# Half of a product behind the next pair's first, transposes one product earlier, an average one step later, seven more tiles of x stored

## The chip, the cores and the metric

The kernel runs on one core of a Trainium2 chip. The metric is the device time of one launch in microseconds (us): the median of several runs. A profiled execution of the same program gives the trace. The core has five engines that run side by side and wait for each other by semaphores: TensorE (PE, matmuls; PEld are its weight loads), VectorE (DVE), ScalarE (ACT), GpSimd (POOL, which here issues the indirect DMAs) and SyncE (SP, which here issues plain DMAs). Each engine takes its instructions in the order in which the program lists them.

## The reference

Sixteen graphs of 1024 nodes with 512 features; one adjacency matrix for all. Attention with 8 heads of 64 over the neighbours of each node, an output projection, a residual sum and a normalisation of each row:

```
q = (x @ Wq + bq).reshape(b, n, H, HD)
k = (x @ Wk + bk).reshape(b, n, H, HD)
v = (x @ Wv + bv).reshape(b, n, H, HD)
scores = jnp.einsum('bqhd,bkhd->bhqk', q, k) / jnp.sqrt(jnp.float32(HD))
scores = scores + (1.0 - adj)[None, None, :, :] * -1000000000.0
attn = jax.nn.softmax(scores, axis=-1)
out = jnp.einsum('bhqk,bkhd->bqhd', attn, v).reshape(b, n, d)
y = out @ Wo + bo
...
x = _layernorm(x + y, axis=-1)
```

x is (16, 1024, 512) and adj is (1024, 1024), zeros and ones, all float32. Most nodes have only a few neighbours; a node with none gets the mean of all v rows of its graph, since its scores are all equally masked.

## The kernel before

**Rows in order of their number of neighbours.** At its start the kernel sorts the 1024 nodes by number of neighbours, and from then on works on x in that order: eight tiles of 128 rows for each graph (a "batch" b), tile t of batch b being number 8b + t. Rows of x come by an indirect DMA on POOL (`gather_x`, L1009).

**Two streams of work.** The first, the *fronts*, is dense and bound to TensorE: it turns x into q, k and v and writes them to DRAM. The second is sparse. For every tile of queries it goes through *blocks*: for each block POOL gathers 128 rows of k and v, one for each query (L1292), VectorE multiplies q with k and sums by head (L1313, L1317), ScalarE takes the exponentials (L1328), ScalarE or VectorE weighs v (L1341, L1345), and the result is added up (L1357, or on TensorE L1366, L1367). There are 530 blocks in all. When a tile is closed, VectorE divides (L1387), TensorE transposes the result o (`turn`, L1401), ScalarE copies it out (L1405), TensorE multiplies it with Wo (`finish`, product po, L799), and then come the residual and the normalisation (`complete`, L1097).

**Steps.** The program is written out by a planner in plain Python, the loop from L1538. One turn of it is a *step*, n, and belongs to one block. `later(k, fn)` puts a piece of work k steps on, and within a step work is written out in a fixed order: exponentials, products, gathers, sums, then what was planned for that step (`plan`), then the *units* of TensorE. Units are taken from the list `finishing` (products po) if there is one, else from `fronts`, while a credit lasts that each step tops up (L1592 to L1618). A unit has a cost, a function, and a condition on which it may be written out; if it isn't ready, the step ends. The list `urgent` holds small TensorE work that goes out in each step after its first unit, as long as there are fronts: the turns of o, and `mean_pe`.

**A pair of tiles.** `pair(b, j)` (L816) makes the front units of tiles 2j and 2j + 1. q is a plain product of four matmuls for each tile (`q0`, `q1`); tile 1 has no q except in the first batch, and tile 0's is made once for two batches. k and v of the two tiles come from a scheme with seven products of half the size in place of eight, on sums and differences of the weights (T1 to T4, made once) and of x (s1 to s4, four VectorE sums L783 to L786 for each pair, `combine`; s1, s2, s3 have one buffer each). The products share three kinds of PSUM banks: x and z have one bank each, p4, p6 and p7 take from a ring of four banks that q, po, the turns and the transposes of x use too. A half of a product is two matmuls, and each float32 matmul shows as two instructions in the trace: a half is "x4". In the order of L994 to L1005:

- x, first half; ScalarE copies it out as e (L969)
- p6; VectorE makes w = p6 + e (L972)
- q of the even tile
- x, second half, on top of the first; ScalarE copies it out as k of the even tile (L835)
- p7; VectorE makes g = p7 + w (L975)
- xt: the transposes of x for the next pair (L757); ScalarE copies them out in the next step (L761), and a step later come the four sums
- z, first half (below: z1); VectorE makes v of the odd tile, v1 = z + g (L984)
- q of the odd tile
- p4; VectorE makes k of the odd tile (L979), and its k and v go to DRAM
- z, second half (below: z2), on top of z1; it may be written out once v1 has been; VectorE makes v of the even tile, v0 = z + w (L988), and its k and v go to DRAM

When both tiles have been sent, VectorE adds their v to a sum (`add_v`, L863). After the last pair of a batch `mean_pe` (L867) averages the sum with one matmul, ScalarE copies the row, SP stores it (L873), and the batch is marked as set up; only then are its blocks gathered.

**Rows stored twice.** The residual of a tile is x itself, in sorted order. For tiles whose numbers are in `STORED`, the x that was loaded for the fronts is written to DRAM (L773, on SP) and loaded from there as the residual (L1035, SP); then the load of x three tiles on, which takes the same buffer, is planned two steps later (L774). For the others the residual is gathered again by POOL (L1038), and the load of x three tiles on follows at once. `SPILL` names tiles whose turned o is put to DRAM and multiplied with Wo at the end.

Of the kernel before, what the change touches and what calls it, by code (L numbers as in the profile page):

```python
# [42 lines left out]
LAZY = 2  # L43

SPILL = (*(8 * b + t for b in range(4, 12) for t in (3, 6)), 45, 69, 93, 102, 103, 106, 107)
STORED = {*SPILL, *(i for i in range(10, 102) if i % 8 in (2, 4, 5, 7)), *(i for i in range(102, 128) if i % 8 > 1)}
LATE = 12

AHEAD_LAST = 11
# [129 lines left out]
def kernel(  # L179
# [75 lines left out]
    with ExitStack() as main:  # L255
# [190 lines left out]
        now, plan, rest, urgent, known, waiting, combined = [0], {}, {}, [], [], [], []  # L446

        def later(k, fn):
            plan.setdefault(now[0] + k, []).append(fn)
# [366 lines left out]
        def pair(b, j):  # L816
# [16 lines left out]
            def out_k(i, p):  # L833
                kv = new_kv(i)
                nc.scalar.copy(kv[:, 0:D], p)  # L835
                later_last(1, lambda: norm(b, tt[i], kv[:, 0:D]))
# [5 lines left out]
            def send(i):  # L842
                assert b < PAIRED_FROM or gathered[0] >= start[max(0, b // 2 * 2 - 2)]
                kv = KV[b, tt[i]]
                rows, base = kv_of(b)
                for lo, hi in ((0, LONE), (LONE + P, 2 * P)) if b and tt[i] == 0 else ((tt[i] * P - (LONE if b and tt[i] == 1 else 0), None),):
                    hi = lo + P if hi is None else hi
                    part = slice(0 if lo % P == 0 or hi - lo == P else LONE, P if hi - lo == P or lo else LONE)
                    later(1, lambda lo=lo, hi=hi, part=part: nc.sync.dma_start(rows[base + lo:base + hi, :], kv[part, :]))
                R["sent"] = R.get("sent", 0) + 1  # L850
                if R["sent"] == 2:
                    later(1, add_v)
                    if j == NT // 2 - 1:
                        later(2 if b else 3, lambda: urgent.append(mean_pe))

            def add_v():
                kv = [KV.pop((b, t))[:, D:] for t in tt]
# [64 lines left out]
            if (b, j) == (0, 0):  # L922
# [12 lines left out]
                units = q0 + q1 + xt  # L935
# [9 lines left out]
            def a(i, h):  # L945
                return XT[b, tt[i]][:, ts(h, HD2)]
# [44 lines left out]
            def s(i):  # L991
                return lambda: SX[b, j][i - 1]
# [3 lines left out]
            units += unit("p6", s(2), T2, True, out_w, None)  # L996
            units += q0
            units += unit("x", lambda: a(0, 1), B21, False, lambda: out_k(0, R["x"]), "e")
            units += unit("p7", s(3), T3, True, out_g, None)
            units += xt  # L1000
            units += unit("z", s(1), T1, True, out_v1, None)
            units += q1
            units += unit("p4", lambda: a(1, 1), T4, True, out_k1, None)
# [512 lines left out]
        with tc.manual_schedule():  # L1516

            fronts += transpose_x(0, 0) + transpose_x(0, 1)
            fronts_by = []
            for b in range(B):  # L1520
                for j in range(NT // 2):
                    fronts += pair(b, j)
                fronts_by.append(sum(u[0] for u in fronts))
            fronts_time = fronts_by[-1]

            def needed(b, part):
                b += int(part)
                if b >= B:
                    return fronts_time
                return fronts_by[b - 1] + (part - int(part)) * (fronts_by[b] - fronts_by[b - 1])  # L1530

            finishing, last_finish, reloads, last_reload = [], -LEAD_IN, 0, 0
            fronts_end = start[B - 1] - 12
            credit = 0.0
            for t in range(3):
                load_x(0, t)
            n = -LEAD_IN
            while n < total or plan or rest or urgent or done or finishing or spilled or lone_tiles or not guarded:  # L1538
                now[0] = n
                if n < 0:  # L1540
                    share = START_SHARE if n > FRONT_BY else LEAD_SHARE if n > -LEAD_IN else TRANSPOSE * 1.5
                elif n >= start[LATE + 1]:

                    share = sum(u[0] for u in fronts) / max(fronts_end - n, 1) + NS * SUM / NBT if fronts else LAST_SHARE
                elif n in start:

                    b = start.index(n)
                    left = sum(u[0] for u in fronts)
                    ahead = EARLY + FIRST * (1 - max(0, b - 1) / LATE)
                    goal = fronts_time - needed(b + 2, ahead / NBT)  # L1550
                    kept = sum(number(b, t) not in SPILL for t in tiles_of(b))
                    share = (max(0.0, left - goal) + kept * NPAIR * PRODUCT + NS * SUM) / (start[b + 1] - start[b])
                if 0 <= n + 3 < total:
                    exponentials(n + 3)
                if 0 <= n + 4 < total:
                    products(n + 4)
                while gathered[0] < min(n + (AHEAD if fronts else AHEAD_LAST) + 1, total) and blocks[gathered[0]][0] in set_up:
                    gather(gathered[0])
                    gathered[0] += 1
                if 0 <= n + 1 < total and not by_act(n + 1):  # L1560
                    weigh(n + 1)
                if 0 <= n < total and blocks[n][2] < OWN[blocks[n][1]]:
                    add_own(n)
                if 0 <= n + 4 < total:
                    scores(n + 4)
                if n - 1 in closes:
                    normalise(*closes[n - 1])
                if 0 <= n < total and blocks[n][1:] == one_key_at(blocks[n][0]):
                    turn(blocks[n][0], ONE_KEY, V1.pop(blocks[n][0]))
                if 0 <= n < total and blocks[n] == (B - 1, *MORE_AT):  # L1570
                    turn(B - 1, MORE_TILE, V1.pop("more"))
                for fn in plan.pop(n, ()):
                    fn()
                if 0 <= n + 2 < total and by_act(n + 2):
                    weigh(n + 2)
                for fn in rest.pop(n, ()):
                    fn()
                credit += paced(share, n) if n >= 0 else share
                if 0 <= n < total and blocks[n][2] >= OWN[blocks[n][1]]:
                    add_up(n)  # L1580
                    credit -= SUM
                for tile_done in done[:0 if fronts and len(done) < LAZY else 1 if fronts else 2] + coming:
                    if tile_done not in loaded and kept_y() < 5:
                        load_y(*tile_done)
                if lone_tiles and kept_y() < 4:
                    load_lone(lone_tiles.pop(0))
                coming[:] = [t for t in coming if t not in loaded]
                if spilled and not fronts and n > last_reload + 1 and len(Y) - kept_y() < 7:
                    reload(*spilled.pop(0), reloads)
                    reloads, last_reload = reloads + 1, n  # L1590
                first_unit = True
                while credit > 0 or urgent:  # L1592
                    if urgent and not (first_unit and fronts):
                        urgent.pop(0)()
                        continue
                    if (
                        not finishing and len(done) > (LAZY if fronts else 0) and n > loaded.get(done[0], n) + 1
                        and n > last_finish + bool(fronts) and not total - 2 <= n < total
                    ):
                        finishing = finish(*done.pop(0))  # L1600
                        last_finish = n
                    units = finishing or fronts
                    if not units:
                        if urgent:
                            urgent.pop(0)()
                            continue
                        break
                    cost, fn, ready = units[0]
                    if ready and not ready():
                        if urgent:  # L1610
                            urgent.pop(0)()
                            continue
                        break
                    del units[0]
                    fn()
                    credit -= cost
                    first_unit = False
                credit = min(credit, 2 * share)  # L1618
                while known and waiting:
                    load_x(*waiting.pop(0))  # L1620
                preps += prep.pop(n, [])
                preps = [g for g in preps if next(g, True) is None]
                n += 1
# [34 lines left out]
```

## Time and profile before

| what | value |
|---|---|
| runs | 1843.5, 1845.46 and 1851.71 us; median 1845.46 |
| profiled execution, its own time | 1842.18 us |
| its span in the trace | 1840.4 us, 25352 instructions |
| granted TensorE clock, mean | 0.996 |
| DMA | 558.54 MB, mean 303 GB/s |

How to read it: the span runs from the first to the last instruction of the trace; the time of the launch lies a little above it. "Busy" is the time in which an engine had an instruction under way. Matmuls overlap in the pipeline, so one shows as 0.59 us while the next starts 0.43 us after it. The slices of the page show TensorE at nine tenths or more from the second slice to the last but one:

```profile
PE   7999999999999999999999999999999999999997
...
DVE  6889889999989999999999999999999999997986
ACT  3637869989889898999889988989799999987886
POOL 1367766766565776767757666677666767665786
```

Each digit is a fortieth of the span, 46 us, in tenths. The costliest groups of TensorE in the page, with count, busy time, mean ns and idle time before them:

```profile
L799 PE MATMUL pq<-wq,xT 128*128 128x512 f32 x792 | 367.8, 596 | 0.0
L799 PE MATMUL po<-wo,oT 128*128 128x512 f32 x792 | 359.3, 594 | 0.7 <-ACT oT L1405 0.7
L956 PE MATMUL x<-b,xT 128*128 128x512 f32 x504 | 237.3, 593 | 0.5 <-ACT e L969 0.4
L956 PE MATMUL pp<-t,s 128*128 128x512 f32 x504 | 237.0, 593 | 0.0
L956 PE MATMUL z<-b,s 128*128 128x512 f32 x252 | 119.2, 596 | 7.0 <-DVE kv L984 7.0
L956 PE MATMUL z<-t,s 128*128 128x512 f32 x252 | 118.6, 593 | 0.0
```

In these names pq and po are the products of q and of the output, pp are p4, p6 and p7, z<-t,s is z1 and z<-b,s is z2, pxT are the transposes of x, poT the turns of o, pm the averages.

### The profile page before, as it was taken

To read this page: it belongs to the slowest core of one execution; us is meant where nothing else is said; L and a number is where in the kernel's file an instruction comes from. 1 tells how busy PE (TensorE), PEld (TensorE's weight loads), DVE (VectorE), ACT (ScalarE), POOL (GpSimd) and SP (SyncE) were. 2 spreads that over 40 slices of the span, in tenths; PEclk is the share of its full clock that TensorE was granted. 3 is DMA by queue.
4 is the path that set the end of the run, shared out by engine and by line. 5 is a ranking of instruction groups with operands and counts; after the bars stand their busy time and mean duration, and the time that the engine had idled before them with its cause. 6 is when DMAs were issued, how large, how long until landed. Compare 5 with 4: busy or idle time off the path is not lost.

```text
span 1840.4 us, 25352 instructions
## 1 busy us (share of the span) xinstructions
PE 1798.2 (98%) x5140; PEld 876.2 (48%) x5140; DVE 1693.7 (92%) x3473; ACT 1563.2 (85%) x6183; POOL 1215.3 (66%) x1142
## 2 busy tenths in 40 slices
PE   7999999999999999999999999999999999999997
PEld 3444454554444454444444445444544444444443
DVE  6889889999989999999999999999999999997986
ACT  3637869989889898999889988989799999987886
POOL 1367766766565776767757666677666767665786
PEclk9999999999999999999999999999999999999998
DMA  7358787989889899999988998999989999889995
GB/s 287 106 190 253 256 325 237 346 301 327 308 280 314 295 336 319 344 316 308 347 316 310 346 335 276 343 321 322 339 315 325 314 355 326 306 324 325 338 319 191
DMA packets 198791, 558.54 MB, mean 303 GB/s; under 512 B 33450, under 2 KB 33470, under 8 KB 198626
## 3 DMA queue, kind: packets, MB, share of 16 engines
q0 software_dynamic: 112640, 370.50, 59.3%
q1 hardware_dynamic: 82910, 180.52, 26.2%
q10 hardware_dynamic: 3076, 5.82, 0.9%
q14 instruction: 122, 1.00, 0.2%
q8 instruction: 43, 0.70, 0.2%
HBM read 420.30 MB, written 157.45 MB: 314 GB/s over the span
## 4 chain that ended last, share of the span: by engine, by line
PE 69%; DVE 10%; ACT 9%; DMA 4%; issue 3%; POOL 1%; SPq 0%; POOLq 0%; DVEq 0%; ACTq 0%
PE po L799 17%; PE pq L799 15%; PE pp L956 12%; PE z L956 9%; PE x L956 9%; ACT pv L1341 5%; DVE qk L1313 2%; PE poT L1401 2%; PE pxT L757 2%; PE sum L1367 2%; DVE s L1317 2%; PE sum L1366 2%; DVE pv L1357 1%; ACT sq_k L809 1%; DMA kvg<-kv_pair,place_row 1%
## 5 line engine op out<-in xcount | busy, mean ns | idle before, releaser
L1341 ACT ACTIVATE pv<-kvg,pv 128x64 f32<-128x64 f32 x3600 | 907.5, 341 | 0.0
L1292 POOL DMA_INDIRECT kvg<-kv_pair,place_row x462 | 526.7, 1140 | 307.4 <-ACT pv L1341 99.6
L799 PE MATMUL pq<-wq,xT 128*128 128x512 f32 x792 | 367.8, 596 | 0.0
L1317 DVE TENSOR_REDUCE s<-qk 128x8 f32<-128x512 f32 x530 | 360.7, 681 | 6.8
L799 PE MATMUL po<-wo,oT 128*128 128x512 f32 x792 | 359.3, 594 | 0.7 <-ACT oT L1405 0.7
L1313 DVE TENSOR_TENSOR qk<-qt,kvg 128x512 f32<-128x512 f32 x434 | 297.2, 685 | 1.1 <-DMA kvg<-kv_rows,key_row 0.6
L956 PE MATMUL x<-b,xT 128*128 128x512 f32 x504 | 237.3, 593 | 0.5 <-ACT e L969 0.4
L956 PE MATMUL pp<-t,s 128*128 128x512 f32 x504 | 237.0, 593 | 0.0
L1357 DVE TENSOR_TENSOR pv<-pv,pv 128x520 f32<-128x520 f32 x329 | 228.3, 694 | 4.3 <-ACT pv L1341 4.2
L799 PEld LDWEIGHTS po<-wo,oT 128*128 128x128 f32 x792 | 149.1, 191 | 170.0 <-issue 160.2
L799 PEld LDWEIGHTS pq<-wq,xT 128*128 128x128 f32 x792 | 148.4, 192 | 161.9 <-issue 149.9
L1010 POOL DMA_INDIRECT x<-in_x_dram,asked_row x120 | 133.0, 1108 | 77.8 <-issue 21.3
L1148 POOL DMA_INDIRECT out_dram<-y,asked_row x129 | 146.9, 1139 | 39.1 <-issue 21.2
L1328 ACT ACTIVATE pv<-s,absent 128x8 f32<-128x8 f32 x434 | 127.0, 294 | 44.0 <-DVE s L1317 40.8
L809 ACT ACTIVATE sq_k<-kv 128x128 bf16<-128x128 f32 x512 | 150.8, 301 | 6.4 <-DVE kv L979 3.4
L956 PEld LDWEIGHTS pp<-t,s 128*128 128x128 f32 x504 | 94.7, 191 | 108.1 <-issue 99.4
L956 PEld LDWEIGHTS x<-b,xT 128*128 128x128 f32 x504 | 94.2, 191 | 107.4 <-issue 99.0
L956 PE MATMUL z<-b,s 128*128 128x512 f32 x252 | 119.2, 596 | 7.0 <-DVE kv L984 7.0
L1246 POOL DMA_INDIRECT qg<-q_rows,query_row x96 | 104.4, 1088 | 28.4 <-issue 26.9
L956 PE MATMUL z<-t,s 128*128 128x512 f32 x252 | 118.6, 593 | 0.0
L956 PE MATMUL pp<-t,xT 128*128 128x512 f32 x252 | 118.5, 593 | 0.0
L1134 ACT ACTIVATE y<-y,stats 128x512 f32<-128x512 f32 (+1 forms) x128 | 102.7, 806 | 17.0 <-DVE stats L1129 17.0
(279 smaller groups left out, 2713.0 us busy)
## 6 DMA issues: line engine op xcount, KB each, us to landing
kv_pair<-kv SPq DMA_DIRECT2D x98, 512.0 KB
q_rows<-q SPq DMA_DIRECT2D x106, 256.0 KB
qt<-q_rows SPq DMA_DIRECT2D x98, 256.0 KB
residual<-x SPq DMA_DIRECT2D x83, 256.0 KB
y<-residual SPq DMA_DIRECT2D x83, 256.0 KB
kv_rows<-kv SPq DMA_DIRECT2D x15, 512.0 KB
kvg<-kv_pair,place_row POOLq DMA_INDIRECT x462, 6.9
kv_pair<-kv SPq DMA_DIRECT2D x28, 256.0 KB
```

The source lines that it names most:

```text
L799: nc.tensor.matmul(p, lhs(c), w[:, c, :], start=(c == 0), stop=(c == NPAIR - 1))
L809: nc.scalar.activation(sq, s[:, ts(h, P)], AF.Square, scale=scale, accum_out=sums[:, h:h + 1])
L956: nc.tensor.matmul(R[bank], l[:, ts(c, P)], right[:, c, :], start=(first and c == 0), stop=(c == 1), skip_group_check=True,)
L1010: nc.gpsimd.indirect_dma_start(out=y, out_offset=None, in_=x_rows, in_offset=bass.IndirectOffsetOnAxis(ap=asked_row[:, t:t + 1], axis=0), ...
L1148: nc.gpsimd.indirect_dma_start(out=out_rows[b, t], out_offset=bass.IndirectOffsetOnAxis(ap=rows, axis=0), in_=y, in_offset=None, element_o ...
L1246: nc.gpsimd.indirect_dma_start(out=q, out_offset=None, in_=q_rows[b % ROWS], in_offset=bass.IndirectOffsetOnAxis(ap=rows, axis=0))
L1292: nc.gpsimd.indirect_dma_start(out=KG[n], out_offset=None, in_=rows, in_offset=bass.IndirectOffsetOnAxis(ap=(place_row if b else key_row)[ ...
L1313: nc.vector.tensor_tensor(QK[n], q, KG[n][:, 0:D], op=OP.mult)
L1317: nc.vector.tensor_reduce(S[n], QK.pop(n).rearrange("p (h d) -> p h d", d=HD), axis=AX.X, op=OP.add)
L1328: nc.scalar.activation(PV[n][:, D:], S.pop(n), AF.Exp, bias=bias)
L1341: nc.scalar.activation(pv[:, ts(h, HD)], v[:, ds(D + h * HD, HD)], AF.Copy, scale=pv[:, D + h:D + h + 1])
L1357: nc.vector.tensor_tensor(PV[b, t], PV[b, t], pv, op=OP.add)
```

## The change

Five edits, all in the planner. The number of matmuls is the same.

1. z2 of a pair is kept back (`held`) and put behind the first unit (the first half of x) of the next pair. The very first pair, which has other units, is put in whole; the last pair's z2 comes at the end.
2. xt stands ahead of p7 rather than behind it.
3. `mean_pe` goes to the urgent list three steps after the last pair's tiles have been sent, in every batch; before, it was two steps in all but the first.
4. With fronts left, urgent work goes out after two units of a step rather than after one.
5. `STORED` has all tiles from 10 on except tiles 0 and 1 of each batch. Numbers 11, 14, 19, 22, 27, 30 and 99 are new; there are 90 in place of 83.

```
-STORED = {*SPILL, *(i for i in range(10, 102) if i % 8 in (2, 4, 5, 7)), *(i for i in range(102, 128) if i % 8 > 1)}
+STORED = {*SPILL, *(i for i in range(10, 128) if i % 8 > 1)}
...
                     if j == NT // 2 - 1:
-                        later(2 if b else 3, lambda: urgent.append(mean_pe))
+                        later(3, lambda: urgent.append(mean_pe))
...
             units += unit("x", lambda: a(0, 1), B21, False, lambda: out_k(0, R["x"]), "e")
+            units += xt
             units += unit("p7", s(3), T3, True, out_g, None)
-            units += xt
             units += unit("z", s(1), T1, True, out_v1, None)
...
-            fronts_by = []
+            fronts_by, held = [], []
             for b in range(B):
                 for j in range(NT // 2):
-                    fronts += pair(b, j)
+                    head, *tail = pair(b, j)
+                    fronts += [head] + held + (tail if (b, j) == (0, 0) else tail[:-1])
+                    held = [] if (b, j) == (0, 0) else tail[-1:]
                 fronts_by.append(sum(u[0] for u in fronts))
-            fronts_time = fronts_by[-1]
+            fronts += held
+            fronts_time = sum(u[0] for u in fronts)
+            fronts_by[-1] = fronts_time
...
-                first_unit = True
+                ahead = 2 if fronts else 0
                 while credit > 0 or urgent:
-                    if urgent and not (first_unit and fronts):
+                    if urgent and ahead <= 0:
                         urgent.pop(0)()
                         continue
...
-                    first_unit = False
+                    ahead -= 1
```

## The prediction

> **What bounds the kernel now.** I read the page's first part, then TensorE's list of waits, then the timelines around the longest of them.
>
> ```profile
> PE 1798.2 (98%) x5140; PEld 876.2 (48%) x5140; DVE 1693.7 (92%) x3473; ACT 1563.2 (85%) x6183; POOL 1215.3 (66%) x1142
> ```
>
> TensorE stands still for 1840.4 - 1798.2 = 42.2 us in all. The change moves TensorE's instructions and drops none, so what it can gain is inside these 42.2 us. Its waits:
>
> ```profile
> PE pxT L757 <- DMA x<-in_x_dram: 7.1, 2, 4.2
> PE z L956 <- DVE kv L984: 7.0, 5, 3.0
> PE pm L867 <- DVE vsum L863: 3.1, 3, 1.9
> PE poT L1401 <- DVE stats L1123: 3.1, 1, 3.1
> PE poT L1401 <- DVE o L1387: 2.6, 1, 2.6
> ...
> PE x L956 <- ACT e L969: 0.4, 1, 0.4
> PE pxT L757 <- DMA x<-in_x_dram,asked_row: 0.4, 1, 0.4
> ```
>
> Columns: total, times, longest. The first is the very beginning of the run and the fourth its very end (1808 us); the change touches neither. Lines two, three and five are what it can reach: 7.0 + 3.1 + 2.6 = 12.7 us, 0.7% of the time.
>
> The five waits of z are the second half of product z (z2), which needs VectorE's v1 (L984) to have emptied the one z bank. Pair by pair in the timeline, four of the five are the first pair of a batch, where the odd tile has no q product, so only p4 (1.72 us) stands between z1 and z2. One of them on TensorE, then on VectorE:
>
> ```profile
> 542.96 1.88 PE L956 MATMUL z<-t,s 128*128 128x512 f32 x4
> 544.68 1.88 PE L956 MATMUL pp<-t,xT 128*128 128x512 f32 x4
> 546.39 0.59 PE L1366 MATMUL sum<-pv,sums 128*128 128x256 f32 x2
> 546.83 0.61 PE L1367 MATMUL sum<-pv,sums 128*128 128x264 f32 x2
> 549.82 1.55 PE L956 MATMUL z<-b,s 128*128 128x512 f32 x3 [2.38 <-DVE kv L984]
> ```
>
> ```profile
> 544.95 0.43 DVE L783 TENSOR_TENSOR s<-xT 128x256 f32<-128x256 f32 x1 [2.96 <-PE z L956]
> ...
> 546.08 0.42 DVE L786 TENSOR_TENSOR s<-xT,s 128x256 f32<-128x256 f32 x1
> 546.42 0.69 DVE L1112 TENSOR_TENSOR y<-po,y 128x512 f32<-128x512 f32 x1
> ...
> 549.08 0.68 DVE L984 TENSOR_TENSOR kv<-z,g 128x512 f32<-128x512 f32 x1
> ```
>
> The four sums of x for the next pair (L783 to L786) overwrite s1, which z1 still reads (one buffer), so VectorE waited 2.96 us for z1, and v1, queued behind them, came late for z2.
>
> **The change part by part.** A product of four matmuls takes 1.72 us from its start to the next one's (542.96 to 544.68). A step is one gathered block: 434 + 96 = 530 of them (L1313) from 120.8 to 1808.3 us, 3.2 us each.
>
> Half of z behind the next pair's x: z2 gets 1.72 us more cover in every pair but the first and the last. Two waits are longer: 3.01 us (at 1065.88) leaves 1.29, 2.38 leaves 0.66; the other three vanish. Saved 7.0 - 1.95 = **5.05**. Ends: 0 (VectorE is later by as much) and 7.0. The price is that v0 (L988), the even tile's store and the sum of v come 1.72 us later.
>
> Average of v at three steps in place of two: the matmul that averages comes 3.2 us later, and its longest wait was 1.9, so **3.1** is saved. Ends 0 and 3.1. Late next is the store of the mean row, and the gathers of that batch, which are released by it. They run many steps ahead except in the last batch:
>
> ```profile
> 1680.77 0.24 SPq L873 DMA_DIRECT2D kv_pair<-mean  x1
> 1681.05 0.80 SPq L1279 DMA_DIRECT2D qt<-q_rows  x2
> ```
>
> There POOL begins at once: a gather of x rows at 1683.04 after 6.71 us of waiting for a store, the first gather of the batch at 1684.88. One step would put the mean at 1684.0, and POOL's gathers 0 to 3.2 us later; most of the step is hidden by that store. I take **+1.0**.
>
> Two units ahead of an urgent one: only the turn of o at 1544.10 (2.62 us) waited. The next unit after it is a half of x, 1.72 us; put ahead of it, **1.72** is saved, ends 0 and 2.6. In exchange every turn comes up to 1.72 us later for ScalarE, which copies it a step later and already waits for turns, 21.3 us in 24 waits; ScalarE has 1840.4 - 1563.2 = 277 us idle, so no cost, and at most 24 x 1.72 = 41 us of ScalarE's own idle time if that cover is gone.
>
> After each of these seven or so stops the second matmul lost another 0.1 us (timeline starts 0.53 apart where 0.43 is usual): **0.7** saved.
>
> x's transposes ahead of p7: the same 8 matmuls, 0.88 us, so p7 is 0.88 us later and x is wanted 1.72 us earlier. The next pair's x, now one product earlier, keeps its distance of 8.6 us to them (p7, z1, q, p4 for z1, q, p4, z2), 5.2 without q. But the sums of x are set two steps behind the transposes, and z1 stays where it is. From z1's end to the first of the sums I read 62 distances: 25 are under one step, and they lack 24.1 us in all to 3.2. A shift by 1.72 us crosses a step's edge in 1.72/3.2 = 54% of cases: 24.1 x 0.54 = 13 us of VectorE waiting for z1. VectorE has 147 us idle; such a wait hurts TensorE where z2 is close, in 15 of 63 pairs: 13 x 15/63 = 3.1 us, and z2 now has 1.72 us more cover, which holds most waits of this size (13 us over some 13 places). I take **+1.0**; ends 0 and 13.
>
> More x stored: seven tiles (11, 14, 19, 22, 27, 30, 99). Each adds two issues to SP (medians 0.39 and 0.44 us: 5.8 us), removes one gather of residual rows from POOL (1.08 us: 7.6 us), and puts the load of x three tiles on two steps (6.4 us) later. For these loads the gather's issue leads the transposes by 16.5 to 49.5 us; landing takes 5.0, so the tightest keeps 16.5 - 6.4 - 1.72 - 5.0 = 3.4 us. POOL also waits for such stores before it refills x (12.4 us over 83): 7 x 12.4/83 = 1.0 us. On SP the reload of y can wait for an output store and hold q's and kv's stores behind it (37.5 us over 83): 3.2 us, where SP idles 747 us for q alone. The write adds 7 x 0.26 = 1.8 MB to 558.5, 0.3%. On TensorE I take **+0.2**; ends -0.4 (its one wait of 0.4 us for such rows) and +3.
>
> Sum: -5.05 - 3.1 - 1.72 - 0.7 + 1.0 + 1.0 + 0.2 = **-8.4 us**. The profiled execution took 1842.18 (span 1840.4): 1833.8. It lies 3.3 us under the median of the runs, 1845.46, so the median is forecast at **1837**.
>
> What a new wait costs besides its own length is seen in three stretches of 40 us:
>
> ```profile
> 1040.00:1080.00 40.00, 36.99 (x112) 18.27 (x111) 37.95 (x72) 36.73 (x153) 25.99 (x25) 1.00 0.94 320
> 1520.00:1560.00 40.00, 37.38 (x114) 18.93 (x113) 39.59 (x74) 36.47 (x148) 29.74 (x27) 1.00 0.93 332
> 1800.00:1840.00 40.00, 26.66 (x67) 12.01 (x65) 24.39 (x80) 25.54 (x69) 23.05 (x25) 0.86 0.45 162
> ```
>
> The figure before the last two is the granted clock: 1.00 around the wait of 3.01 us, 0.86 at the end, where waits of up to 3.1 us came close together. By the row a single new wait costs its own length, and the sum counts it so. [...]
>
> **Rivals.** (1) VectorE takes over: the waits move instead of going. For it: around 1544 VectorE is busy 39.59 of 40 us, so a TensorE that gets ahead there only meets it later. Against: in the stretch of 1066 it has 2 us free, and around 549 it was itself waiting. If only the waits before 1000 us go (1.72, some 1.2 for the smaller ones, less the added 0.2), 2.7 us are gained: 1843.
>
> (2) Slower: the sums of x, a step earlier, wait for z1 (s1 has one buffer, L783). For it: 549.82 above, where 2.38 of VectorE's 2.96 us, 80%, reached TensorE. Against: it was one case of 62, and a first pair. If all 25 close places lose the step and 80% arrives, 19.3 us stand in place of the 1.0: -8.4 + 18.3 = +9.9, so 1855. It decides from 9.4 us of such waits reaching TensorE.
>
> (3) Better: everything in reach goes, 12.7 + 0.7, and nothing is added: 1832.
>
> **How the numbers follow.** 0.5% is 9.2 us and about what a measurement of this kernel tells from no change; the bounds are 1836.2 and 1854.7. The forecast has 0.46 and a range of its own from 1833 to 1841; its centre lies almost on the bound, and I put 0.27 of it below, 0.19 within. Rival (3) has 0.09, rival (1) 0.19, rival (2) 0.26, of which 0.22 is beyond the upper bound, since new waits also shift later steps. Faster 0.27 + 0.09 = 0.36, same 0.19 + 0.19 + 0.04 = 0.42, slower 0.22. The range goes from 1829, three under rival (3), to 1856, which just holds rival (2)'s centre: about 0.05 and 0.13 are left outside.
>
> **What would show it.** In the profile after: TensorE's waits for L984 near 2 us, for L863 near 0, for L1387 near 1, and its idle time near 34 us. VectorE's wait of L783 for z shows the price: 3.0 us before, about 15 if my estimate holds, over 20 for rival (2). ScalarE's wait for turns should grow without TensorE waiting for ScalarE more. x's gathers should not appear among TensorE's waits. The prediction is wrong if new waits stand where I have none, above all for PSUM banks (product lines waiting for VectorE) or in the last 150 us, where the mean row is one step later.

## The result, and the profile after

The changed kernel takes 1859.44 us (median of six runs, 1855.94 to 1861.4), the kernel before 1847.18 in six runs (1843.5 to 1851.71). The ratio is 1.0065, 95% interval 1.0051 to 1.008: 12.3 us slower, where 1837 was forecast with a range up to 1856. The profiled execution took 1861.17 us, its span is 1859.4, 19.0 more than before.

The page's first part and then TensorE's waits (total, times, longest), after:

```profile
PE 1806.0 (97%) x5127; PEld 876.0 (47%) x5140; DVE 1695.3 (91%) x3473; ACT 1565.1 (84%) x6183; POOL 1204.4 (65%) x1135
```

```profile
PE pp L956 <- DVE y L1112: 4.6, 2, 3.0
PE z L956 <- DVE kv L984: 3.7, 3, 1.4
...
PE pp L956 <- DVE w L972: 2.1, 2, 1.8
PE x L956 <- ACT xT L761: 1.8, 1, 1.8
...
PE pp L956 <- ACT oT L1405: 1.7, 1, 1.7
PE po L799 <- ACT sq_hat L898: 1.5, 1, 1.5
PE pp L956 <- DVE ee L711: 1.5, 1, 1.5
PE pm L867 <- DVE y L1112: 1.4, 1, 1.4
```

VectorE and ScalarE do the same work as before; TensorE stands still for 53.4 us in place of 42.2, and its busy time is 7.8 us longer with the same matmuls, which in places follow each other more slowly (0.85 us in place of 0.43, below). The count of 5127 in place of 5140 is the trace's: 13 records are missing from it, and a second profile of this kernel has 5140. The wait for L863 is gone from the list, that for L1387 too, and that for L984 fell from 7.0 to 3.7. In their place stands a wait that wasn't there at all: pp, with releasers that have nothing to do with its operands. L1112 adds a residual to a product po, and L1405 copies a turned o. What pp shares with them is the ring of four PSUM banks. The longest of these waits, on TensorE and then on VectorE:

```profile
645.50 1.88 PE L799 MATMUL po<-wo,oT 128*128 128x512 f32 x4
647.22 0.60 PE L757 MATMUL pxT<-ident,x 128*128 128x128 f32 x4
647.75 1.02 PE L867 MATMUL pm<-vsum,mean 128*1 128x512 f32 x2
648.70 0.66 PE L757 MATMUL pxT<-ident,x 128*128 128x128 f32 x4
652.39 3.78 PE L956 MATMUL pp<-t,s 128*128 128x512 f32 x4 [3.03 <-DVE y L1112]
655.96 2.95 PE L956 MATMUL z<-t,s 128*128 128x512 f32 x4
```

```profile
651.65 0.68 DVE L1112 TENSOR_TENSOR y<-po,y 128x512 f32<-128x512 f32 x1
...
656.21 0.69 DVE L975 TENSOR_TENSOR g<-pp,w 128x512 f32<-128x512 f32 x1 [3.04 <-PE pp L956]
```

Count the tiles in the ring: po, pxT, pm, pxT, and p7 is the fifth, so it takes po's bank. Three short tiles lie between, 2.1 us of TensorE; po's last matmul ended at 647.38, and VectorE, busy with earlier work, read it only from 651.65 to 652.33; p7 began at 652.39. The same holds at 1488.41, where p7 waited 1.79 us: the fourth tile back is p6, and its reader (L972) ended at 1488.36. Before the change p7 came ahead of the transposes, and what followed them was z1, with a bank of its own.

The second line to see is VectorE's wait for z1, 3.0 us once before:

```profile
DVE s L783 <- PE z L956: 26.7, 11, 6.1
```

To add up the loss I took, from the starts of TensorE's matmuls in the traces, the time from one start to the next beyond the usual pitch (0.429 us at 512 columns, 0.109 at 128, and so on), by what comes next. The stretch runs from the tenth z1 to the last one, some 1415 us, which leaves out the start and the tail. "Half clock" is the excess inside a run of equal matmuls that follow each other at twice the pitch. Most later runs are given in the same columns (us):

```
kernel                           p7    z2   x    turns averages half clock  all gaps  stretch
before                           0.1   7.3  0.7   3.2    4.5       0.0        20.7     1414.5
changed                         10.2   5.2  2.6   0.0    2.6       2.1        36.7     1428.9
changed, second profile         10.7   5.4  2.5   0.1    2.6       1.3        34.7     1428.5
transposes alone                 9.1  25.8  3.1   9.7   11.3       9.3        79.9     1472.0
all but the transposes           0.0   1.4  5.9   2.1    3.2       0.4        29.6     1421.8
half of z alone                  0.0   0.6  7.5   4.2    6.7       0.4        28.0     1420.1
urgent after two alone           0.0   8.0  3.9   3.6    5.4       2.1        33.1     1425.3
all but transposes and urgent    0.2   0.5  6.0   2.4    1.9       0.4        21.0     1414.9
half of z and average            0.2   0.5  6.0   3.0    1.9       0.8        24.8     1417.1
transposes ahead of x's half     1.8  25.6  1.7  21.0    1.2       8.0        99.9     1493.6
changed, sums a step later      11.2   0.3  2.1   0.1    2.9       3.0        40.5     1434.4
changed, z1 ahead of p7          3.1   7.6  2.5   2.5    1.9       0.4        36.1     1428.4
changed, urgent after one       12.4   6.1  2.7   2.5    1.9       0.8        43.3     1435.4
changed, transposes split        0.5   0.5  2.5   0.8    2.6       0.4        22.8     1415.1
split, urgent after one          0.9   1.8  2.1   3.7    1.9       0.4        21.9     1414.2
changed, two buffers for s1      9.8   0.6  2.5   1.1    2.6       2.1        31.3     1423.5
```

The gaps account for the stretch nearly in full: 36.7 - 20.7 = 16.0 against 14.4 for the change. Of the 19.0 us of span, 14.4 lie here, 1.3 before it and 3.3 behind it. p7 has gained 10.1, the half clock 2.1 and x 1.9; z2 gives back 2.1, the averages 1.9, the turns 3.2. That is 6.9 net. The rest of the 16.0 is spread over gaps that have no column here, among them the po of the list above, which waited 1.5 us for a bank too. Four waits make up 8.7 of p7's 10.2 us, so the loss comes from a few places and not from every pair.

### The profile page after: what moved, and what is told of

Same layout as the page of the kernel before. It is cut to its first block, busy times and chain, and to the rows that moved or that the text cites. A ratio compares the mean times of both kernels' runs of the same rounds, so it can differ in the third digit from the quotient of the medians.

```text
span 1859.4 us, 25320 instructions
## 1 busy us (share of the span) xinstructions
PE 1806.0 (97%) x5127; PEld 876.0 (47%) x5140; DVE 1695.3 (91%) x3473; ACT 1565.1 (84%) x6183; POOL 1204.4 (65%) x1135
## 5 line engine op out<-in xcount | busy, mean ns | idle before, releaser
L956 PE MATMUL pp<-t,s 128*128 128x512 f32 x504 | 240.4, 600 | 11.4 <-DVE y L1112 4.6
L809 ACT ACTIVATE sq_k<-kv 128x128 bf16<-128x128 f32 x512 | 151.1, 303 | 7.0 <-DVE kv L979 7.0
L956 PEld LDWEIGHTS pp<-t,s 128*128 128x128 f32 x504 | 90.6, 191 | 101.6 <-issue 80.9
## 6 DMA issues: line engine op xcount, KB each, us to landing
q_rows<-q SPq DMA_DIRECT2D x106, 256.0 KB
qt<-q_rows SPq DMA_DIRECT2D x98, 256.0 KB
residual<-x SPq DMA_DIRECT2D x90, 256.0 KB
y<-residual SPq DMA_DIRECT2D x90, 256.0 KB
kv_pair<-kv SPq DMA_DIRECT2D x28, 256.0 KB
```

The source lines that it names most:

```text
L809: nc.scalar.activation(sq, s[:, ts(h, P)], AF.Square, scale=scale, accum_out=sums[:, h:h + 1])
L956: nc.tensor.matmul(R[bank], l[:, ts(c, P)], right[:, c, :], start=(first and c == 0), stop=(c == 1), skip_group_check=True,)
```

## The experiments

Runs were made in five series, each beside the kernel before. In one series it took 1873 us, in others 1845, 1864 and 1872, so only ratios inside a series are compared, and the table above serves across them: the two profiles of the changed kernel, whose spans differ by 17.3 us, agree in the stretch to 0.4 us and in all gaps to 2.0.

The ratio of whole runs and the stretch of one trace don't always say the same. Three kernels of the first series are shorter by the ratio than by the stretch: all but the transposes (4 to 5 us under before by the ratio, 7.3 over it in the stretch), half of z alone (2 under, 5.6 over) and urgent work after two units alone (5 over, 10.8 over). No trace of the kernel before is kept from that series, so where the difference lies isn't shown. For the kernels that decide below (the changed kernel with urgent work after one unit, with its transposes split, with two buffers for s1) the two measures agree within 3 us.

Three theories. A: the place of the transposes makes the loss, by p7's bank (A1) or by the sums of x, which now overtake z1 and wait for it (A2). B: the moved half of z makes it. C: urgent work after two units makes it.

### One edit alone, and all but one

Transposes alone (edit 2 of the change, nothing else):

```
+            units += xt
             units += unit("p7", s(3), T3, True, out_g, None)
-            units += xt
```

> The kernel before with one edit: x's transposes ahead of p7. Theory A (the place of the transposes makes the loss: VectorE's sums of x come a step earlier and wait for z1, and p7, right behind two short transposes, meets a PSUM bank that is not yet emptied): VectorE's wait of L783 for z over 15 us (3.0 before, 26.7 after), TensorE's waits of pp (p7, p6) for other engines over 5 us (0 before, 11.4 after), time 8 to 15 us over before. Theory B (z's second half, one product later, makes the loss, since v0, the stores and the sum of v come later): time within 3 us of before. Theory C (urgent work after two units makes it): within 3 us of before, too.

1.0302 (1.0273 to 1.0331): 58 us slower, about four times the most that theory A expected. TensorE's waits in its trace:

```profile
PE z L956 <- DVE kv L984: 18.6, 11, 4.2
...
PE pm L867 <- DVE vsum L863: 8.5, 7, 2.3
PE poT L1401 <- DVE o L1387: 6.9, 3, 3.4
```

The late sums (VectorE's L783 waited 28.2 us for z, where it waited 3.0 before) make VectorE late for everything behind them, and the three waits that the other edits shorten are the ones that grow. In the full change those edits cover most of the damage of this one.

All but the transposes:

```
-            units += xt
             units += unit("p7", s(3), T3, True, out_g, None)
+            units += xt
```

(against the changed kernel)

> The changed kernel with x's transposes back behind p7; the four other edits stay. Theory A: most of the loss goes, time between 6 us under before and 3 us over it; the wait of L783 for z back under 6 us, waits of pp under 2 us. Theories B and C: the loss stays, 8 us or more over before, and for C ScalarE's waits for turns stay near 50 us (21.3 before).

0.9975 (0.9958 to 0.9993): by the ratio the loss is gone and a little more; in the stretch half of it is still there (1421.8 us, 1414.5 before, 1428.9 changed). p7 no longer waits in the stretch, though waits of pp come to 3.4 us where under 2 was expected. No large gain is left, and a new wait stands in its place:

```profile
PE x L956 <- ACT xT L761: 4.4, 4, 1.8
```

With z2 moved, the next pair's x comes one product sooner after its transposes, and ScalarE's copy of xT isn't ready. That is what the moved transposes were good for: x waits 5.9 us without them, 2.6 with them.

Half of z alone (edit 1):

> The kernel before with one edit: half of z behind the next pair's first half of x. Theory A: z's waits for L984 fall from 7.0 to some 2 us, time 3 to 5 us under before. Theory B: 5 us or more over before, with VectorE or SP late for v0, its store and the sum of v.

0.9988 (0.9971 to 1.0004). z2's gaps fall from 7.3 to 0.6, more than forecast, but x's rise from 0.7 to 7.5 and the turns' and averages' by 3.2 together. No theory of a loss fits, so B falls; theory A's 3 to 5 us aren't there either.

Urgent work after two units alone (edit 4):

> The kernel before with one edit: urgent work after two units of a step. Theory C: ScalarE's waits for turns rise from 21.3 to over 40 us and the time is 5 us or more over before. Theory A: ScalarE's waits for turns rise all the same, but the time stays within 3 us of before, since ScalarE has 277 us idle.

1.0028 (1.0009 to 1.0047): 5 us slower (10.8 in the stretch), as C has it, but ScalarE's waits for turns only rose to 25.0 us, so the cause that C names isn't seen; nothing in the table is large alone (x 3.2 more, half clock 2.1).

Three edits, without transposes and urgent work:

> The kernel before with three of the edits: half of z behind the next x, the average one step later, more x stored; transposes and urgent work as before. By theory A, and since urgent work after two units cost 5 us when it was alone: 4 to 9 us under before, better than all four edits without the transposes (4 us under). By theory B, which holds the moved half of z at fault: at or over before.

0.9983 (0.9964 to 1.0002): not told from no change, less than theory A expected. z2 and the averages gain 9.4, x loses 5.3.

Half of z and the average:

> The kernel before with two edits: half of z behind the next x, the average one step later. All but the transposes and the urgent work gave 0.17% with more x stored; if storing more is free, this gives the same within 2 us; against half of z alone (0.12%) the averages' waits of some 4.5 us should be gone: 2 to 5 us under before.

1.0001 (0.9992 to 1.001), where 2 to 5 us under before were expected. The averages' gaps are down to 1.9, and the time hasn't moved; their part is no larger than what the others lose.

### Where the transposes stand

The changed kernel itself, beside the next two:

> The changed kernel unaltered, on the chip that the next three run on, so that each is read beside it. If the loss is the kernel's own and not one chip's: 8 to 16 us over before, with 1859.44 against 1847.18 as the measure.

1.0065 (1.0042 to 1.0089), the same as in its first six runs.

One place further ahead:

```
+            units += xt
             units += unit("x", lambda: a(0, 1), B21, False, lambda: out_k(0, R["x"]), "e")
-            units += xt
             units += unit("p7", s(3), T3, True, out_g, None)
```

> The changed kernel with x's transposes one place further ahead, in front of the second half of x. Theory A1 (the bank: p7 takes the fourth next bank of the ring right behind two transposes of 0.44 us, before the reader of that bank is done): 1.72 us of another bank's work now stand between, so TensorE's waits of pp fall from 11.4 to under 5 us and the time falls by 4 us or more against the changed kernel. Theory A2 (the sums of x wait for z1, which reads s1): the sums come 1.72 us earlier still, so VectorE's wait of L783 for z rises from 26.7 to over 40 us and the time rises by 4 us or more.

1.0461 (1.0422 to 1.0499), 90 us over before, 75 over the changed kernel. Both expectations on the waits came true: p7's gaps fell from 10.7 to 1.8, and VectorE's list is led by

```profile
DVE s L783 <- PE z L956: 74.9, 21, 7.5
```

The time went the way of A2, whose mechanism is real and costly where the sums overtake z1 far enough. The whole 75 us aren't A2's, though: the transposes themselves also waited, mostly for banks (28.2 us of gaps, 0.7 in the changed kernel).

Sums of x one step later:

```
-                        later(1, combine)
+                        later(2, combine)
```

> The changed kernel with the four sums of x one step later, so that they no longer overtake z1. Theory A2: the wait of L783 for z falls from 26.7 to under 5 us, and with it most of the loss, 8 us or more. Theory A1: that wait falls all the same, but TensorE's waits of pp stay near 11 us and the time stays within 4 us of the changed kernel. For both: if the next pair's x is not ready because of it, steps end early and TensorE waits where nothing is named.

1.0094 (1.006 to 1.0128), slower than the changed kernel. The wait of L783 for z fell from 26.7 to 2.5 us and z2's gaps to 0.3, but p7 kept 11.2, and p6 of the next pair, which needs a sum (L785), now waited 7.1 for it (4.1 in the stretch). This told against A2 as the whole cause without settling it.

z1 ahead of p7:

```
             units += xt
-            units += unit("p7", s(3), T3, True, out_g, None)
-            units += unit("z", s(1), T1, True, out_v1, None)
+            units += unit("z", s(1), T1, True, lambda: None, None)
+            units += unit("p7", s(3), T3, True, out_g, None)
```

with `out_v1()` as the last line of `out_g`.

> The changed kernel with z1 and p7 exchanged behind the transposes (x's transposes, z1, p7; VectorE makes v1 right after g). The transposes stay where the change put them, but z1, which has a bank of its own, now stands between them and p7, and the sums of x find s1 read. Theory A1 (p7's bank): TensorE's waits of pp fall from 11 to 20 us to under 5 us, and the loss of 15 us against before goes, time from 6 us under before to 4 over it. If something else in the place of the transposes makes the loss (x wanted earlier, ScalarE's copies earlier): 8 us or more over before still.

1.0075 (1.0052 to 1.0098). p7's gaps fell to 3.1 as A1 has it, but the loss stayed, which by the expectation speaks for something else in the place of the transposes. The run has a cost of its own, however: p7 reads s3, which has one buffer as well, and VectorE's sums now waited 11.4 us for pp; v1, bound to p7, came later and z2 waited 7.6. So it decides nothing between A1 and A2.

The same with urgent work after one unit:

> As the run before, with urgent work after one unit again. Theory A1 with the reading that urgent work after two units costs something of its own (5 us alone): 2 to 6 us under the run before and 3 to 9 us under the kernel before. If urgent work after two units helps beside the other edits: slower than the run before.

1.0085 (1.006 to 1.011): slower than the run before, by less than the intervals tell apart; its stretch, 1438.1 us, is 9.7 longer.

One tile's transposes ahead of p7, the other's behind it:

```
-            units += xt
+            units += xt[:1]
             units += unit("p7", s(3), T3, True, out_g, None)
+            units += xt[1:]
```

> The changed kernel with one tile's transposes ahead of p7 and the other's behind it. Theory A1: p7 no longer follows two short users of the ring, so TensorE's waits of pp fall under 5 us; the sums of x start with the second tile, so they come as late as before and L783's wait for z is under 5 us as well; time from 6 us under before to 4 over it. If the loss came with x being wanted earlier: about half of it stays, 6 to 9 us over before.

1.0018 (0.9996 to 1.0039): the loss is gone, with p7 at 0.5, z2 at 0.5 and x at 2.5 us of gaps. So the first tile's x being wanted earlier is not the fault; the second tile's place is. L783 no longer waits for z, either: both A1 and A2 are removed by it.

The changed kernel with urgent work after one unit:

> The changed kernel with urgent work after one unit again, the transposes still ahead of p7. Theory A1 with the reading that urgent work after two units falls in between the transposes and p7 and so tightens the ring: TensorE's waits of pp fall by half, time 4 to 10 us under the changed kernel. If the transposes alone make the loss, or if urgent work after two units shields TensorE from late turns of o: within 3 us of the changed kernel, or over it.

1.0108 (1.0082 to 1.0134) against 1.0065: with the transposes moved, urgent work after two units is worth some 8 us by the ratios, 6.5 by the stretch. Turns wait 2.5 us where they waited 0.0, p7 about 2 more, and the rest is spread; the averages don't show it (1.9).

### Bank or buffer

A second buffer for s1 takes A2 away and leaves the order alone:

```
-bufs=1 + i // 4) for i in (1, 2, 3, 4)]
+bufs=2 if i in (1, 4) else 1) for i in (1, 2, 3, 4)]
```

The first try made room by one scratch buffer for ScalarE's squares (L809) in place of two, among others.

> The changed kernel with two buffers for s1 (the room comes from two small tiles that share one, and from one scratch buffer of ScalarE's squares in place of two); the order of the work is the changed kernel's. The sums of x no longer wait for z1. Theory A2 (sums waiting for z1): VectorE's wait of L783 for z falls to under 3 us, z2's waits for L984 fall under 2 us, and the time falls by 8 us or more against the changed kernel. Theory A1 (p7's bank): p7's waits stay at 8 to 12 us, and the time falls by at most 5 us, what z2 still waited.

1.0169 (1.0153 to 1.0184), spoiled by that scratch buffer (last section). The same in the split kernel, without and with it:

> One tile's transposes ahead of p7, the other's behind it, urgent work after one unit, the other edits as in the change. If urgent work after two units only costs when p7 doesn't follow the transposes (7 to 10 us of TensorE's gaps in the runs without the transposes' move): 3 to 8 us under the split run, 2 to 7 under before. If it helps beside the split: slower than before.

> As the run before, with two buffers for s1. The split has already put the sums behind z1, so theory A expects nothing more from the second buffer: within 2 us of the run before.

0.9991 (0.9982 to 0.9999) without and 1.0067 (1.0054 to 1.0081) with it, where no difference between the two was expected: the price of the scratch buffer. The first of the two is some 1.5 us under before, where 2 to 7 were expected. Beside the changed kernel with urgent work after one unit (1.0108, stretch 1435.4) it differs in the second tile's place alone, and by the ratios and the stretch (1414.2) that place is worth 20 to 21 us. The second try keeps both scratch buffers:

> The changed kernel with two buffers for s1 and the squares' two scratch buffers left as they were (in the earlier run with one, ScalarE's squares took 0.43 us from start to start in place of 0.29, some 70 us of ScalarE, which spoiled it). The room comes from three small tables of the start that share one tile. Theory A2 (sums waiting for z1): time at least 8 us under the changed kernel, that is within 4 us of before or under it. Theory A1 (p7's bank): the sums' wait for z1 and z2's waits go, p7's waits stay at 8 us or more, and the time stays 6 to 14 us over before.

1.0055 (1.0041 to 1.0069), 11.5 us over before. The lines have moved by two here: in its VectorE list the sum that overwrites s1 (L785) no longer waits for z, and z2's gaps are 0.6. The sum that overwrites s3 now waits for a late p7, and TensorE's list still has p7's waits:

```profile
DVE s L786 <- PE pp L958: 4.9, 2, 3.0
DVE s L785 <- ACT xT L763: 4.4, 4, 1.8
```

```profile
PE pp L958 <- DVE y L1114: 4.6, 2, 3.0
...
PE pp L958 <- ACT oT L1407: 1.7, 1, 1.7
```

In the stretch this parts the two: of the 14.4 us, 9.0 stay without the sums' wait for z1, and p7's gaps and the half clock are 9.8 + 2.1. Some 5.4 us were A2's, seen as 4.6 in z2. The time of whole runs shows little of these 5.4 (1.0055 against 1.0065, in different series): the stretch begins at 256.0 us here and at 251.2 in the changed kernel, and why is not known. No run gave the ring a fifth bank, so p7's share rests on what is left here, on the readers that ended just before p7 began, and on the split.

The split kernel with the tiles stored as before:

> The split run with urgent work after one unit, and the tiles stored as in the kernel before. If storing seven more tiles is free, as the prediction had it: within 2 us of the same run with them, some 1 us under before. If it costs: 3 us or more under that run.

0.9995 (0.9983 to 1.0007) against 0.9991 with seven more: storing them costs nothing that shows. The split kernel with urgent work after one unit, 1844.15 against 1845.49, is 0.1% under the kernel before; the lowest ratio is that of all but the transposes, 0.9975, and no version here beats the kernel before by as much as 0.5%.

## Why the prediction was wrong

**What bounds the kernel** was read rightly: all of the loss inside the stretch is TensorE's gaps, while VectorE's work grew by 1.6 us and ScalarE's by 1.9, and GpSimd's shrank.

**The step that failed** is "x's transposes ahead of p7". It was costed by order and distance: p7 0.88 us later, the sums nearer to z1, one microsecond taken, 13 as the upper end. It left out that the transposes and p7 draw on one ring of four banks. A transposed tile uses up a bank in 0.44 us where p4, p6 or p7 takes 1.72, so p7 behind two of them, and often behind a turn or an average as well, asks for the bank of a tile written about 2 us before. The code says so (all take `fill_psum`, four banks), and the prediction named PSUM banks only in its last sentence, as a sign of being wrong; that sign is the one that appeared. What it cost: 10.1 us of gaps and 2.1 us of half clock. The next pair's x, said to keep its distance to the transposes, also waits 2.6 us where it waited 0.7.

**The sums of x against z1.** VectorE's wait of L783 was estimated at about 15 us and was 26.7, which is rival (2)'s sign, "over 20". But rival (2) let 80% of it reach TensorE; with the second buffer 5.4 us went, about a fifth of 26.7. The rival had the direction and nearly the time, 1855, by a mechanism that made only a smaller part; that it came so near is luck. The 80% came from one case of the trace.

**Half of z.** Forecast -5.05, with z2's waits for L984 falling from 7.0 to 2; they fell to 3.7, a saving of 3.3, because the late sums hold up v1. With half of z alone the cover did more than forecast (0.6 us of gaps left), so the cover itself wasn't sized too high.

**The average** was put at -3.1, and the wait for L863 is gone as forecast. But one average now waits 1.4 us for a bank of the ring (pm, L1112), so the gaps fell by 1.9; in the kernels where the transposes weren't moved they fell by 1.3 to 2.6. A small loss of some 0.09 us ahead of each average stays throughout.

**Urgent work.** Forecast -1.72 for turns: they gained 3.2. The reading that this edit costs nothing was wrong by itself (5 us alone by the ratio), and so was the reading that it is independent: beside the moved transposes it saves 6.5 to 8 us.

**More x stored**, +0.2: within what the runs can tell. **The last batch and the tail**, +1.0: 3.3 us behind the last z1, but other kernels show 0.3 to 6.5 there without a pattern by edit, so the share of the later average stays open.

**The sum** took the edits one by one, each against the trace before. The runs show that they aren't independent: the transposes cost 58 us alone, and beside the others 17 by the ratios (1.0065 against 0.9975, in different series) or 7 by the stretch (1428.9 against 1421.8). Even with the upper end for the new waits, 13 us in place of 1.0, the sum would have given +3.6 and not +12.3, and that bound belonged to the sums' waits alone.

The prediction read from its rows that a new wait costs its own length. One of them cost more: the clock dropped inside the fronts. Windows of the changed kernel; the last figures are granted clock, DMA share and GB/s:

```profile
640.00:680.00 40.00, 36.97 (x102) 17.74 (x101) 35.22 (x70) 33.74 (x136) 23.32 (x23) 0.91 0.90 307
1040.00:1080.00 40.00, 39.63 (x115) 19.02 (x114) 39.45 (x77) 36.24 (x146) 26.34 (x24) 1.00 0.92 322
```

After the wait at 652.39 the matmuls of p7 and z1 followed each other at 0.85 us in place of 0.43, and the granted clock from 652 to 659 us is 0.56. The seven steps from the start of p7 to that of z1's last matmul (652.39 to 658.32) took 5.93 us where 3.00 is usual: 2.9 us on top of a wait that was 3.03 us long by the list and 3.2 by the starts. Length alone doesn't decide. In the kernel before, z2's wait of 2.38 us at 549.82 left the clock at 1.00 (549 to 556 us), as did the one of 3.01 at 1065.88 (1065 to 1072). In the tail of the changed kernel a turn's wait of 2.74 us at 1827.65, shorter than that, was followed by a granted clock of 0.76 (1827 to 1834). What does decide, no run here shows.

## What to carry to other kernels

Before an instruction is moved, list what it takes from a shared ring, and who frees it: here a tile of transposes used up a bank in 0.44 us where half a product took 1.72, and the product behind them paid, 10.2 us of p7's gaps in place of 0.1. The waits that named a releaser with no part in the operands pointed to a bank here (p7's for L1112, up to 3.0 us) or to a buffer (L783's for z, 26.7 us in all); find the tile that had it before, and see whether its reader ended just ahead. Edits that shorten the same waits should be costed together, and the one that makes another engine late should be tried alone, since the others may only be covering it (the transposes: 58 us alone, 17 beside the others).

## What the runs showed of the hardware that was not expected

One scratch buffer in place of two for ScalarE's squares, which nobody reads, made each square with its readout take 0.433 us from start to start in place of 0.292 (medians over 512 of them). ScalarE's timeline in the run with one buffer:

```profile
1085.72 0.33 ACT L811 ACTIVATE sq_k<-kv 128x128 bf16<-128x128 f32 x1
1085.93 0.21 ACT L811 ACTIVATION_READ_ACCUMULATOR sq_k<-kv 128x1 f32 x1
1086.17 0.31 ACT L811 ACTIVATE sq_k<-kv 128x128 bf16<-128x128 f32 x1
```

and in the kernel before, with two:

```profile
1060.69 0.30 ACT L809 ACTIVATE sq_k<-kv 128x128 bf16<-128x128 f32 x1
1060.89 0.20 ACT L809 ACTIVATION_READ_ACCUMULATOR sq_k<-kv 128x1 f32 x1
1060.98 0.30 ACT L809 ACTIVATE sq_k<-kv 128x128 bf16<-128x128 f32 x1
```

With one buffer the next square begins after the readout has ended rather than while it runs; 512 x 0.14 is 72 us of ScalarE. The split kernel's time rose by 0.76% with it (1.0067 against 0.9991), beside the second buffer for s1 and some shared tables of the start. The two runs of the changed kernel with two buffers for s1 show the same: 1.0169 with one scratch buffer, 1.0055 with two, and one more shared table as the only other difference.

The kernel before took from 1845 to 1873 us in different series, on one chip too. In the two profiles of the changed kernel the stretch begins at 251.2 and at 270.0 us, so the difference lies ahead of it, most of it between 110 and 250 us from the start. There TensorE shows single waits of up to 14.2 us in the traces of these series; what makes them was not tried.
